# Last triangle stage: row sums on ScalarE, a given share of products for GpSimd, and a new word order

## The chip, the core and the metric

The kernel runs on one core of a Trainium2 chip. The metric is the time of one execution on the device in microseconds (us). The engines are TensorE (PE in the profile; PEld its weight loads), VectorE (DVE), ScalarE (ACT), GpSimd (POOL), and SyncE (SP), which issues most DMAs. Each works through its own instructions in program order and waits on semaphores for the others.

## The reference

Four images x of 64 x 64 x 256 go through two layers. Only the second layer's last image is touched by the change.

```python
# layer 0, per image of 4096 tokens
f, g, v = xt @ Wf + bf, xt @ Wg + bg, xt @ Wh + bh
x = x + softmax(g f^T) v @ Wo + bo
# layer 1, "triangle": 8 heads of 32, N = 64
scores = einsum('bilhd,bljhd->biljh', q, k) / sqrt(32)
att = softmax(scores, axis=2)                       # over l
out = einsum('biljh,bilhd,bljhd->bijhd', att, v1, v2)
h = layer_norm(x + out.reshape(...) @ Wo)
x = layer_norm(relu(h @ W1 + b1) @ W2 + b2 + h)
```

## The kernel before

The whole program is one list of instructions in an order written out by hand (`tc.manual_schedule()`, L1714). For each image b = 0 to 3 `layer0` (L527) makes the attention, the projections q, k, v1, v2 and the first triangle step, and then `first_layer1` (b = 0) or `next_layer1` (L1588, b = 1 to 3) makes the triangle stage. After b = 3, `Tokens.alone` (L1379) does the token work (heads, two layer norms, the two-layer perceptron) of the last image by itself; the token work of image b - 1 runs inside the triangle stage of image b.

**Steps and words.** A triangle stage has 32 steps: four pairs of heads, and eight groups of eight rows i for each. Two steps, 2i and 2i + 1, are one round of the word list. `next_layer1` goes through the list `ORDER_LAST` (for b = 3; `ORDER` for b = 1, 2) once in each of 20 periods, L1690 to L1707. A word `R14/2` is read so: letter, step of the round (1: the odd one), number, and how many periods late it is: in period p it is done for round i = p - 2. A word without a slash is for round i = p. The words, with their engine:

- `R` + step + m: product m of 8, `product` (L1067, instruction at L1078): the weights of one row and one head times v2, 128 x 2048. m of `8 - npool(step)` and above go to GpSimd (tile Rp, 2 buffers, weights from attP), the others to VectorE (tile R, 3 buffers, weights straight from att in PSUM).
- `A` + step + m: `accumulate` (L1081, L1088): TensorE sums product m over l into one of two accumulators `acc` of the step; four matmuls. It frees the R or Rp buffer.
- `T` + step + half: `take` (L1095): ScalarE copies an accumulator to SBUF; after the second one SP issues the step's eight stores.
- `S`, `W`, `V`, `t`, `c` + step: `sums` (L991: VectorE adds up the softmax rows at L1003 unless the step is in `summed`, and takes reciprocals, L1005), `weights` (L1009: ScalarE scales rows, 8 activations), `stationary` (L1051: ScalarE puts v1 into wsel; then SP loads v1 of step + 2), `turn_weights` (L1026: TensorE transposes, tile att), `copy_weights` (L1035: ScalarE copies GpSimd's part to attP).
- `K` + step: `row_sums` (L981): ScalarE makes the same row sums with 8 activations that accumulate, at L986. It is used in the first image's list, `ORDER0`, only.
- `sp`, `sf`, `e0`, `e1`, `f0`, `f1`: TensorE's scores of the next pairs (L964), and ScalarE's exponentials of them (L974); `sf` and `f` for i = 0, the others for i = 1 to 11. After that no scores are made.
- Token words of a piece q: `h0`, `h1` heads (L1196; SP then loads tiles A and yt of the next piece), `sa` statistics on VectorE (L1221), `rr` and `pp` root on ScalarE and polish on GpSimd, `fa` and `fo` affine on ScalarE (L1283), `ht` transposes on TensorE, `hT` and `hU` copies of them on ScalarE (L1311), `m0`, `m1` hidden layer on TensorE (L1339), `r0`, `r1` rectify on ScalarE (L1348), `z0`, `z1` second layer on TensorE (L1359), `so` its statistics on ScalarE (L1237, L1241), `fi` the end on GpSimd (L1373, L1374) and the output's DMA on SP.

The accumulators and the scores share two PSUM buffers (`pa`), the tiles mp, zp, hp and htp two others (`pb`). When a tile is allocated it takes the buffer that was given free first in program order, and its first writer waits for that buffer's last reader.

`npool` gives GpSimd 3 products in even and 2 in odd steps for b > 0, and goes by the string `ON_POOL` for b = 0. In the stage of b = 3 there is an exception at L1695: in the period of step 0, `A05` is left out where it stands and is done right after A04, where the list has `A04`.

```python
            if step not in self.summed:
                nc.vector.tensor_reduce(den, rows, AX.X, ALU.add)
```

Of the kernel before, what the change touches and what calls it, by code (L numbers as in the profile page):

```python
# [52 lines left out]


ORDER_LAST = """
    r0/1 A10/2 A11/2 m1/1 R14/2 R05/1 S1/1 R15/2 T10/2 sp/1 A14/2 A16/2 r1/1 e0/1 e1/1 A15/2 A05/1 T11/2 R04/1
    A04/1 z0/1 W1/1 R03/1 V1/1 fi/2 S0 z1/1 t1/1 so/1 R06/1 R00/1 c1/1 sa A03/1 R07/1 R02/1 A06/1 A02/1 A00/1
    rr/1 pp/1 W0 R01/1 A07/1 A01/1 fo/1 fa T01/1 R12/1 t0 T00/1 R17/1 h1/-1 sf/1 R13/1 h0/-1 f0/1 ht f1/1 R16/1
    hU A13/1 hT A12/1 A17/1 R11/1 c0 R10/1 m0 V0
""".split()  # L60


# [14 lines left out]


ON_POOL = "33232323332323233323232332232323"


@with_exitstack
def attention_then_triangle_kernel(
# [7 lines left out]
    NB = x.shape[0]  # L91
# [815 lines left out]
    class Layer1:  # L907
# [45 lines left out]
        def scores(self, pair, u):  # L953
            if u == 0:
                self.S[pair] = big.tile([P, N, N], F32, tag="S", name="S", bufs=2)
            qk = self.qk[pair]
            q = qk[0].rearrange("p (i l) -> p l i", l=32)
            k = qk[1].rearrange("p (l j) -> p l j", j=N)
            sp = pa("sp").rearrange("p o (l i) -> p o l i", i=N)
            for n in range(8):  # L960
                for h in range(2):
                    for lh in range(2):
                        rows = slice(64 * lh + 32 * h, 64 * lh + 32 * h + 32)
                        nc.tensor.matmul(  # L964
                            sp[ts(h, 64), lh, n, :], k[rows, u * 8 + n, :], q[rows, u * 8 + n, :],
                            start=True, stop=True,
                        )
            self.sp = (pair, u, sp)

        def take_scores(self, *halves):  # L970
            pair, u, sp = self.sp
            for lh in halves or (0, 1):
                l0 = lh * 32 + u * 8
                nc.scalar.activation(  # L974
                    self.S[pair][:, :, l0 : l0 + 8].rearrange("p i l -> p l i"), sp[:, lh],
                    AF.Copy if self.safe else AF.Exp,
                )
# [38 lines left out]
        def npool(self, step):  # L1016
            if self.b == 0:
                return int(ON_POOL[step])
            return 3 - step % 2


# [499 lines left out]
    def words_of(order):  # L1521
        for w in order:
            w, late = (w.split("/") + ["0"])[:2]
            yield w, int(late)
# [63 lines left out]
    def next_layer1(b, L, rest, ahead, F):  # L1588
        own = b == NB - 1
        t0 = NP * (b - 1)  # L1590
# [97 lines left out]
        step_word, scores, take_scores, _ = step_words(L, fetched, was_stored, spread)  # L1688
        mps[1] = {}
        for period in range(NP + 4):  # L1690
            if period == 1:
                L.owed()
            for word, late in words_of(ORDER_LAST if own else ORDER):
                i = period - late
                if own and i == 0 and word in ("A05", "A04"):  # L1695
                    for m in (4, 5) if word == "A04" else ():
                        step_word("A", 0, m)
                elif word[0] in "RATSWVtc":
                    step_word(word[0], 2 * i + int(word[1]), int(word[-1]))
                elif word in ("sp", "sf"):  # L1700
                    if (i == 0) == (word == "sf"):
                        scores(i)
                elif word in ("e0", "e1", "f0", "f1"):
                    if (i == 0) == (word[0] == "f"):
                        take_scores(i, int(word[1]))
                else:
                    of_piece(word, i)  # L1707
# [4 lines left out]
    def run(safe):  # L1712
        rest, ahead = Tokens(), Ahead()
        with tc.manual_schedule():  # L1714
            F = front0(0)
            for b in range(NB):
                L = layer0(b, F, safe, rest, ahead)
                F = Front() if b + 1 < NB else None
                if F is None:

                    rest.ios.append(L.io)
                if b == 0:
                    first_layer1(L, ahead, F)
                else:
                    next_layer1(b, L, rest, ahead, F)
                if F is not None:
                    rest.ios.append(L.io)
            rest.alone(NP * (NB - 1), NP * NB)
# [50 lines left out]
```

## Time and profile before

| what | value |
|---|---|
| median of 4 runs | 3605.39 us (3602.74 to 3607.36) |
| profiled execution, its time | 3606.98 us |
| its span, first to last instruction | 3605.1 us (1.9 us lie around it) |
| mean granted TensorE clock | 0.992 |
| busy share PE, PEld, DVE, ACT, POOL | 97%, 52%, 79%, 55%, 49% |

Busy microseconds by stage (windows of the same profile):

| stage | window, us | PE | DVE | ACT | POOL |
|---|---|---|---|---|---|
| triangle, b = 2 | 2130 to 2550 | 415.1 | 392.3 | 274.8 | 368.6 |
| attention, b = 3 | 2550 to 3000 | 442.9 | 318.1 | 209.6 | 76.9 |
| last triangle stage | 3000 to 3450 | 444.2 | 431.2 | 306.2 | 425.8 |
| of it, with scores | 3050 to 3325 | 275.0 | 266.1 | 194.1 | 264.0 |
| of it, without | 3325 to 3436 | 107.4 | 110.4 | 70.3 | 108.0 |
| tokens alone | 3450 to 3605 | 140.6 | 114.8 | 82.4 | 0 |

A busy share says how much of a window an engine was at work, not whether the others waited for it. For that one looks at the distance from one round of the word list to the next, at what each engine's idle time was ended by, and at the chain of work that ended last. The start of an instruction on one engine, set beside the end of the one it waited for on another, gives the cost of a handover.

### The profile page before, as it was taken

The page shows a single profiled execution, that of the slowest core. Times are in us where ns is not written, and L with a number is a line of the kernel's source. Part 1 is how long each engine was busy: PE and PEld are TensorE (multiplying, and loading weights), DVE is VectorE, ACT ScalarE, POOL GpSimd, SP SyncE. Part 2 cuts the span into 40 slices and gives each one's busy share as a digit, 9 for nine tenths or more (in the row PEclk, how much of TensorE's full clock was granted, in tenths as well). Part 3 has the DMA queues.
Part 4 walks back from the last instruction along what each step waited for, and adds up shares of the span by engine and source line. Part 5 has one row for each costly group of instructions (what it writes and reads, how often), then busy time and mean ns, then how long its engine had stood idle before and what let it go on. Part 6 is the DMA issues. An engine that isn't in the chain of part 4 may idle for free.

```text
span 3605.1 us, 59264 instructions
## 1 busy us (share of the span) xinstructions
PE 3509.1 (97%) x22218; PEld 1888.7 (52%) x22218; DVE 2837.1 (79%) x2620; ACT 1983.3 (55%) x4733; POOL 1755.9 (49%) x899
## 2 busy tenths in 40 slices
PE   8999999898999999999999999999999999999998
PEld 6555444444555555554555555554455555555477
DVE  4777499896555579999777749999787766999987
ACT  3444477664444366665444456666444436777655
POOL 5000099894000068889011128889511106999920
PEclk9999999999999999999999999999999999999999
DMA  9444565464222354425422264343633345341221
GB/s 171 135 134 129 131 155 144 112 148 111 68 75 69 110 133 108 109 63 107 104 91 91 76 158 103 93 100 77 126 96 103 96 110 140 92 97 46 66 69 57
DMA packets 514105, 378.60 MB, mean 105 GB/s; under 512 B 320593, under 2 KB 455505, under 8 KB 504977
## 3 DMA queue, kind: packets, MB, share of 16 engines
q1 hardware_dynamic: 464768, 347.76, 35.2%
q0 software_dynamic: 36160, 19.94, 5.4%
q10 hardware_dynamic: 12880, 7.01, 0.7%
q8 instruction: 178, 2.92, 0.3%
q14 instruction: 119, 0.97, 0.1%
HBM read 207.82 MB, written 166.72 MB: 104 GB/s over the span
## 4 chain that ended last, share of the span: by engine, by line
PE 82%; POOL 7%; DVE 5%; issue 4%; ACT 2%; DMA 1%; SPq 0%; ACTq 0%; DVEq 0%; POOLq 0%
PE o L609 24%; PE acc L1088 19%; PE proj L692 8%; PE s L582 7%; POOL Rp L1078 5%; PE mp L1339 4%; PE zp L1359 4%; PE sp L964 3%; PE v1p L724 2%; PE hp L1196 2%; PE y L661 2%; PE att L1030 1%; DVE R L1078 1%; PE vp L388 1%; PE v1p L462 1%
## 5 line engine op out<-in xcount | busy, mean ns | idle before, releaser
L1078 POOL TENSOR_TENSOR Rp<-attP,v 128x2048 f32<-128x2048 f32 x323 | 1469.1, 4580 | 407.4 <-DMA k<-k 301.5
L1078 DVE TENSOR_TENSOR R<-att,v 128x2048 f32<-128x2048 f32 x701 | 1556.1, 2279 | 67.0 <-PE acc L1088 41.1
L609 PE MATMUL o<-e,v 128*128 128x512 f32 x2048 | 1045.8, 594 | 0.0
L594 ACT ACTIVATE e<-s 128x1024 f32<-128x1024 f32 x512 | 523.0, 1023 | 529.9 <-PE s L582 446.3
L582 PE MATMUL s<-gT,fT 128*128 128x512 f32 x1024 | 788.7, 772 | 16.3 <-ACT e L594 10.9
L616 DVE TENSOR_TENSOR esum<-esum,e 128x2048 f32<-128x2048 f32 x224 | 512.4, 2287 | 305.0 <-ACT e L594 303.2
L1088 PE MATMUL acc<-R,wsel 128*32 128x512 f32 x5608 | 709.5, 602 | 19.3 <-DVE R L1078 8.4
L609 PEld LDWEIGHTS o<-e,v 128*128 128x128 f32 x2048 | 389.0, 190 | 278.1 <-issue 234.9
L1098 ACT COPY ao<-acc 128x1024 f32<-128x1024 f32 x256 | 256.7, 1011 | 259.9 <-PE acc L1088 211.9
L1088 PE MATMUL acc<-Rp,wsel 128*32 128x512 f32 x2584 | 338.0, 595 | 23.6 <-POOL Rp L1078 22.0
L1088 PEld LDWEIGHTS acc<-R,wsel 128*32 128x32 f32 x5608 | 158.2, 110 | 373.4 <-issue 276.7
L1373 POOL TENSOR_TENSOR hz<-hz,log_bc 128x512 f32<-128x512 f32 x32 | 45.7, 1427 | 599.4 <-ACT hz L1283 599.4
L582 PEld LDWEIGHTS s<-gT,fT 128*128 128x128 f32 x1024 | 195.0, 191 | 252.4 <-issue 233.6
L1013 ACT ACTIVATE es<-S,rd 128x64 f32<-128x64 f32 x1024 | 258.2, 337 | 27.2 <-DVE rd L1005 24.9
L1267 POOL TENSOR_SCALAR nt<-mv 128x2 f32<-128x2 f32 (+1 forms) x49 | 9.4, 192 | 510.4 <-DVE mv L1222 505.3
L1339 PE MATMUL mp<-hT,w 128*128 128x256 f32 x1024 | 244.8, 384 | 1.7 <-ACT hT L1311 1.7
L1359 PE MATMUL zp<-w,hid 128*128 128x256 f32 x1024 | 240.0, 385 | 2.5 <-ACT hid L1348 2.1
L1359 PEld LDWEIGHTS zp<-w,hid 128*128 128x128 f32 x1024 | 187.9, 190 | 50.1 <-issue 14.7
L1339 PEld LDWEIGHTS mp<-hT,w 128*128 128x128 f32 x1024 | 185.1, 190 | 54.8 <-ACT attP L1038 12.6
L638 DVE RECIPROCAL rec<-den 128x512 f32<-128x512 f32 x32 | 107.4, 3358 | 116.2 <-PE den L634 110.8
L1088 PEld LDWEIGHTS acc<-Rp,wsel 128*32 128x32 f32 x2584 | 79.9, 110 | 219.0 <-issue 151.0
L974 ACT ACTIVATE S<-sp 128x512 f32<-128x512 f32 x128 | 131.0, 1093 | 66.9 <-PE sp L964 66.8
(199 smaller groups left out, 3782.6 us busy)
## 6 DMA issues: line engine op xcount, KB each, us to landing
v<-v2d SPq DMA_DIRECT2D x44, 512.0 KB
v1c<-v1d SPq DMA_DIRECT2D x128, 128.0 KB
aT<-ao SPq DMA_DIRECT2D x1024, 16.0 KB
A<-aT SPq DMA_DIRECT2D x256, 64.0 KB
hz<-raw SPq DMA_DIRECT2D x32, 512.0 KB
y<-yT SPq DMA_DIRECT2D x56, 256.0 KB
q<-st SPq DMA_DIRECT2D x56, 256.0 KB
k<-st SPq DMA_DIRECT2D x52, 256.0 KB
```

Source lines behind the costliest of these rows:

```text
L582: nc.tensor.matmul(s_ps[r // 2][:, r % 2, :], fT[tt][:, ts(r * 4 + n, P)], gT[qb // 4][:, ts(qb % 4, QB)], start=True, stop=not safe,)
L594: nc.scalar.activation(e[g][:, 2 * j : 2 * j + 2, :], s_ps[j], AF.Exp)
L609: nc.tensor.matmul(o_ps[qb], F.v[tt][:, r * 4 + n, :], es[:, r, :], start=(k == 0 and r == 0), stop=(k == 7 and r == 3),)
L616: nc.vector.tensor_tensor(esum[qb], esum[qb], es, ALU.add)
L692: nc.tensor.matmul(ps, w[:, cc, rows], y(qb, cc), start=(cc == 0), stop=(cc == 1))
L974: nc.scalar.activation(self.S[pair][:, :, l0 : l0 + 8].rearrange("p i l -> p l i"), sp[:, lh], AF.Copy if self.safe else AF.Exp,)
L1013: nc.scalar.mul(e[:, i, :], rows[:, i, :], rec[:, i : i + 1])
L1078: eng.tensor_tensor(R, src.unsqueeze(1).to_broadcast([P, D, N]), v2[h], ALU.mult)
L1088: nc.tensor.matmul(acc[32 * c : 32 * c + 32, n % 2, :], w[:, n, c, 16 * h : 16 * h + 32], R[:, ts(c, 8), :].rearrange("p d j -> p (d j)"), ...
L1098: nc.scalar.copy(self.ao[step][:, ts(np, 2)].rearrange("p k d j -> p k (d j)"), self.acc[step][np])
L1339: nc.tensor.matmul(self.mp[:, fc % 2, :], w1_sb[:, cc, ts(fc, P)], self.hT[tt][:, cc, :], start=(cc == 0), stop=(cc == 1),)
L1359: nc.tensor.matmul(zp[:, n, :], self.hid[tt][:, fc, ts(n, P)], w2_sb[:, fc, :], start=(fc == 0), stop=(fc == 3 and tt not in self.hT2),)
```

## The change

Three things change, all in the stage of b = 3. The list `ORDER_LAST` is a new one; it has the words K0 and K1, so that steps 1 to 31 get their row sums from ScalarE (step 0 is done in `layer0`, as before); the heads h0 and h1 are no longer made one period early. `npool` goes by a new string, 79 products in all instead of 80. The exception for `A05` and `A04` is gone. The number of all other instructions stays.

```diff
 ORDER_LAST = """
-    r0/1 A10/2 A11/2 m1/1 R14/2 R05/1 S1/1 R15/2 T10/2 sp/1 A14/2 A16/2 r1/1 e0/1 e1/1 A15/2 A05/1 T11/2 R04/1
-    A04/1 z0/1 W1/1 R03/1 V1/1 fi/2 S0 z1/1 t1/1 so/1 R06/1 R00/1 c1/1 sa A03/1 R07/1 R02/1 A06/1 A02/1 A00/1
-    rr/1 pp/1 W0 R01/1 A07/1 A01/1 fo/1 fa T01/1 R12/1 t0 T00/1 R17/1 h1/-1 sf/1 R13/1 h0/-1 f0/1 ht f1/1 R16/1
-    hU A13/1 hT A12/1 A17/1 R11/1 c0 R10/1 m0 V0
+    R14/2 A12/2 A17/2 c0/1 hU/1 R16/2 R05/1 K0 m0/1 m1/1 A11/2 A16/2 S1/1 R04/1 A14/2 R15/2 S0 V0/1 r0/1 R01/1
+    T10/2 A05/1 A04/1 W1/1 A15/2 K1 r1/1 R07/1 h0 R02/1 h1 T11/2 z1/1 V1/1 z0/1 W0 R00/1 R06/1 t1/1 fi/2 so/1
+    A02/1 A01/1 A07/1 A06/1 A00/1 sa c1/1 rr/1 R03/1 pp/1 T01/1 A03/1 sf/1 T00/1 sp fa R10/1 R13/1 t0 f1/1 f0/1
+    e1 ht e0 hT A10/1 R12/1 A13/1 R17/1 R11/1 fo/1
 """.split()
...
 ON_POOL = "33232323332323233323232332232323"
+ON_POOL_LAST = "32323322332323232323213232332322"
...
         def npool(self, step):
             if self.b == 0:
                 return int(ON_POOL[step])
+            if self.b == NB - 1:
+                return int(ON_POOL_LAST[step])
             return 3 - step % 2
...
             for word, late in words_of(ORDER_LAST if own else ORDER):
                 i = period - late
-                if own and i == 0 and word in ("A05", "A04"):
-                    for m in (4, 5) if word == "A04" else ():
-                        step_word("A", 0, m)
-                elif word[0] in "RATSWVtc":
+                if word[0] in "RATKSWVtc":
                     step_word(word[0], 2 * i + int(word[1]), int(word[-1]))
```

## The prediction

> **What bounds the kernel now.** First the table of stages (columns: window, its length, then busy microseconds of PE, PEld, DVE, ACT, POOL, clock, DMA share, GB/s). Only the last triangle stage, about 3000 to 3450 us, is touched; one row from its middle and one from its end:
>
> ```profile
> 3225.00:3250.00 25.00, 25.00 (x240) 13.23 (x232) 24.10 (x19) 18.53 (x51) 23.86 (x14) 1.00 0.59 135
> ...
> 3375.00:3400.00 25.00, 24.12 (x176) 11.31 (x177) 24.93 (x16) 17.24 (x52) 24.35 (x14) 1.00 0.33 82
> ```
>
> TensorE has no gap in the middle; at the end VectorE and GpSimd have none. Next the chain that ended last (start, duration, what), to see how long one period of the word list is and who sets it:
>
> ```profile
> 3050.57 0.86 PE hp L1196 x4
> ...
> 3078.33 0.86 PE hp L1196 x4
> ...
> 3353.65 6.80 POOL Rp L1078 x2
> ...
> 3380.84 6.80 POOL Rp L1078 x2
> ```
>
> The period is 27.76 while scores (`sp`) are made, all on PE; without scores it is 27.19, on POOL, though PE's work is 1.91 less (25.85). So in the middle relief of VectorE buys nothing; an order that is cheaper for PE does.
>
> Then the timelines of PE, DVE and ACT, for the handovers:
>
> ```profile
> 3155.67 1.07 PE L1088 MATMUL acc<-R,wsel 128*32 128x512 f32 x8
> 3156.55 1.04 PE L1088 MATMUL acc<-Rp,wsel 128*32 128x512 f32 x8
> ...
> 3159.99 1.04 PE L1088 MATMUL acc<-R,wsel 128*32 128x512 f32 x8
> 3160.96 0.66 PE L1030 MATMUL att<-ident,es 128*128 128x128 f32 x4
> ```
>
> ```profile
> 3156.80 13.28 DVE L1078 TENSOR_TENSOR R<-att,v 128x2048 f32<-128x2048 f32 x6 [0.35 <-PE acc L1088]
> ...
> 3327.78 8.88 DVE L1078 TENSOR_TENSOR R<-att,v 128x2048 f32<-128x2048 f32 x4
> ...
> 3348.10 15.45 DVE L1078 TENSOR_TENSOR R<-att,v 128x2048 f32<-128x2048 f32 x7
> ```
>
> ```profile
> 564.22 0.26 ACT L986 ACTIVATE S<-S 128x64 f32<-128x64 f32 x1
> 564.37 0.20 ACT L986 ACTIVATION_READ_ACCUMULATOR S<-S 128x1 f32 x1
> 564.46 0.25 ACT L986 ACTIVATE S<-S 128x64 f32<-128x64 f32 x1
> ```
>
> An accumulation costs PE 0.86 from start to start, 0.97 before another kind. A03's matmuls end at 3156.55; R01, which needs its buffer, starts 0.25 later. Four products take VectorE 8.88, seven 15.45 (2.21 each). A product that is done is used 0.03 later (R02: 3348.10 + 2.29 = 3350.39, A02 at 3350.42). A row sum on ScalarE takes 0.24, accumulator read included: 1.92 a step.
>
> **Row sums.** 31 reductions leave VectorE (0.71 to the next start; step 0's stays): 1.42 a period; a period without waits goes from 27.1 to 11 x 2.21 + 1.16 (bn_stats) + 0.24 (reciprocals) = 25.7. ScalarE gains 3.84 a period: 70.6% of 27.76, or 19.6, becomes 23.4. Queued behind the K words are r0, T10, W1 and r1; I walk them below.
>
> **GpSimd's share.** 79 products instead of 80, five in every period but one, which has four. Its loop stays 5 x 4.55 + 2.60 (finish) + 1.85 (polish) = 27.2.
>
> **PE's new order.** A12 A17 m0 m1 A11 A16 A14 A05 A04 A15 h0 h1 z1 z0 t1 A02 A01 A07 A06 A00 A03 sp t0 ht A10 A13, then A12 again. The accumulations stand in three runs instead of four (0.11 less) and m0, m1 stand together: sixteen of their matmuls in the last stage take 3.46 (3466.92 to 3470.38), so an m costs 1.73 and 1.92 only before another kind (0.19 less); the z pair comes after transposes, 1.95 each as the second is now (3153.19 to 3155.14), 0.10 less in all. Sum: runs 3.55 + 5.29 + 5.29, m 3.65, h 2.16, z 3.90, sp 1.91, t and ht 1.52 = 27.3 with scores, 25.4 without.
>
> A rule speaks on PE's share. The Trainium skill, "Perfetto Trace Analysis", Identifying the Most-Contended Engine, says that matmul busy time is no measure of the distance to the limit and that weight-load busy time is better; in the first row above that is 13.23 of 25, which would leave PE about half free. The trace sides with it in part only: the 0.11 and 0.19 show that "100%" can shrink, but the starts lie end to end. By the rule alone PE would drop out of the sum and GpSimd's 27.2 would be the period.
>
> **The new tightest loop.** VectorE's products run R14, R05 or R15 with R04, R01, R02, R00, bn_stats, R03, R10, R13, R12, R11. With three R buffers, R03 in the built program waits for A02's last matmul. From A02's end: 0.25, R03 R10 R13 R12 8.88, 0.03, so A12 can start at 9.16. PE's own way there (A01 A07 A06 A00 A03 sp t0 ht A10 A13) is 9.0 with scores, 7.1 without. From A12's start to the next A02's end: 0.86 + 0.97 + 3.65 + 5.29 + 2.16 + 3.90 + 0.53 + 0.86 = 18.2. The loop is 27.4, **with or without scores**. bn_stats is not in it: h1 is done 5 us before A02's end.
>
> Walked through it, counting from A02's end: ScalarE ends fa at 6.4 (ht can then start at 6.6; with scores it comes at 6.8), fo at 10.3 (m0 at 11.0), T10 at 16.7 (A05 at 17.2), r1 at 21.3 (z1 at 22.0), W0 at 25.1 (t0 a period on at 33.7). GpSimd polishes at 1.4 to 3.3, R17 to 7.8 (A17 at 10.0), R16 to 12.4 (A16 at 15.5), R05 or R15 to 16.9 (A05 17.2, A15 18.9), and ends finish 1.1 into the next period: 0.2 spare. In periods with R15 on GpSimd, R04 waits for A11 and is ready as A04 wants it (18.1): nothing spare. SP's queue keeps all its issues, 14.5 of 27.4 (two stores of about 5.2, tiles A and yt 2.5, others 1.4); the output leaves at about 1.5 and lands by 5, hU needs its buffer at 10.4; A and yt have 25 us to land.
>
> **Start.** Step 1's sum waits for ScalarE: K1 begins where W1 now does (3005.26), ends 3007.2, and R04, queued behind that reciprocal, starts 4.4 later than now. PE does A05 first (GpSimd's product, ready 3007.67), A04 at 3009.7, then z1, z0, t1, which cover the delay of W1; K0, K1 and W0 lie under them. A02 of pair 0 ends at 3016.1 instead of 3015.8: +0.3. To A02 of pair 1: 27.3 + 1.9 (two scores) + 0.3 (R03) = 29.5, now 31.4: -1.9. If the z words did not cover, the bound is the whole 4.4 later start; the other bound is 0.
>
> **Periods.** Ten with scores: 10 x (27.4 - 27.76) = -3.6. Four without: 4 x 27.4 = 109.6 against 107.6 now (3324.0 to 3431.6): +2.0. VectorE's relief is eaten by the wait for A02.
>
> **End.** Now 17.4 from the last A02 (3432.5) to the heads of the next stage (3449.91). New: 9.16 + 0.86 + 0.97 + 3.65 + 3.55 + 1.73, the last for piece 17's heads, which are no longer made early: 19.9: +2.5. Their statistics then follow at once, so the next stage's first hidden matmul waits about 0.6 longer.
>
> Sum: 0.3 - 1.9 - 3.6 + 2.0 + 2.5 + 0.6 = -0.1. The profiled execution (3606.98 with span 3605.1) would become 3606.9; on the median of the runs, 3605.39, I forecast **3605.3**. About 0.2%, 7.2 us, is what a measurement of this kernel can tell from no change.
>
> **Rivals.** *Slower: VectorE's loop is longer than I have it.* R03's buffer comes one accumulation later (A01), or handovers add as much: for it, VectorE idles about 1.7 before R03 in every period and two loops have nothing spare; against it, the wait in the built program. It costs 0.86 x 14 = 12: **3617**. It decides from 0.5 a period (7.2 / 14). GpSimd gets there too if a product takes 0.15 more than 4.55 (27.95). Chance 0.20.
> *Faster: PE's work alone sets the pace.* Then 10 x (27.3 - 27.76) - (107.6 - 4 x 25.4) = -4.6 - 6.0, end 0 instead of +2.5: sum -11.6: **3594**. For it, VectorE has 1.4 less; against it, three buffers. Chance 0.12.
> *The change does not do what it says*: the dispatch list now has K, and 31 reductions are gone from the built program; were they still there, each period would be 1.4 fuller on VectorE, inside its idle time: about 3605. Chance below 0.02, counted with the forecast.
>
> Forecast case 0.68. Unknown terms: loop 14 x 0.15, start 1.5, end 1.5, so about 3 either way alone; to leave out no more than 2 in 10 the range goes part of the way to both rivals: **3598 to 3614**. Faster by over 0.2% 0.12, within 0.68, slower 0.20.
>
> **What would show it.** Heads to heads 27.4 in both halves of the stage; VectorE waiting about 1.7 for PE before R03 every period; PE waiting about 2 at A12 once the scores are gone; reductions 97 to 66, 248 more row-sum activations on ScalarE, GpSimd products 323 to 322; the next stage starting within 3 us of 3450. Periods above 27.9, or a wait of PE at A04, A05, z1 or ht, would make me wrong on the slow side; periods near 25.4 without scores on the fast side.

## The result, and the profile after

| | before | after |
|---|---|---|
| median, us | 3605.81 (60 runs, 3602.74 to 3608.25) | 3610.05 (40 runs, 3606.27 to 3613.36) |
| ratio | | 1.0012, 95% interval 1.0007 to 1.0016 |
| profiled execution: time, span | 3606.98, 3605.1 | 3612.13, 3610.3 |

The time is inside the range on record and within 0.2%. But the change is slower by more than the interval of its ratio, and I had forecast no change (a sum of -0.1). So the sum is wrong by about 4 us in the medians and by 5.3 in the two profiles, and the question is which terms were wrong.

The change did what it says: VectorE's reductions went from 97 to 66, ScalarE's row-sum activations from 248 to 496, GpSimd's products from 323 to 322, and the next stage starts at 3452.7.

Now the two windows that were shown of before. Columns: window, length, busy time of PE, PEld, DVE, ACT, POOL, clock, DMA share, GB/s:

```profile
3225.00:3250.00 25.00, 25.00 (x242) 12.60 (x240) 22.94 (x16) 20.45 (x68) 23.95 (x14) 1.00 0.63 134
3375.00:3400.00 25.00, 23.38 (x177) 10.90 (x176) 22.99 (x17) 18.77 (x77) 24.01 (x15) 1.00 0.42 110
```

VectorE is relieved as intended (24.10 to 22.94, and 24.93 to 22.99) and ScalarE has the work. TensorE still has no gap in the middle, and at the end now no engine is full: a sign that a chain over several engines sets the pace there. Its length is read from the heads (PE's timeline of after, first instruction of each pair):

```profile
3231.39 1.13 PE L1199 MATMUL hp<-wo,A 128*128 128x256 f32 x4
...
3259.00 1.13 PE L1199 MATMUL hp<-wo,A 128*128 128x256 f32 x4
...
3286.61 1.13 PE L1199 MATMUL hp<-wo,A 128*128 128x256 f32 x4
...
3315.61 1.13 PE L1199 MATMUL hp<-wo,A 128*128 128x256 f32 x4
...
3343.17 1.13 PE L1199 MATMUL hp<-wo,A 128*128 128x256 f32 x4
```

The period is 27.61 or 27.56 in both halves (before: 27.76 with scores, on average 26.9 without), and one period is 29.00. Which of the two it is follows the string of GpSimd's share: 27.61 where GpSimd has R15, so that VectorE makes R05 ahead of R04, and 27.56 where GpSimd has R05. PE's and VectorE's timelines show A02, and behind it the predicted wait before R03, in brackets behind the instruction:

```profile
3155.26 1.92 PE L1091 MATMUL acc<-R,wsel 128*32 128x512 f32 x16
```

```profile
3156.39 15.48 DVE L1081 TENSOR_TENSOR R<-att,v 128x2048 f32<-128x2048 f32 x7 [1.92 <-PE acc L1091]
```

A02 (the first eight of the sixteen) starts at 3155.26 and ends 0.88 later; R03 follows after 0.25. So the loop that I named exists. Without scores one sign came out otherwise than I had written: TensorE's wait stands at ht, for ScalarE's h, and not at A12 (PE's timeline):

```profile
3357.28 0.66 PE L1309 MATMUL htp<-ident,h 128*128 128x128 f32 x4 [1.47 <-ACT h L1286]
...
3359.94 1.06 PE L1091 MATMUL acc<-R,wsel 128*32 128x512 f32 x8 [0.15 <-DVE R L1081]
```

A12 still starts 9.19 after A02's end (I had 9.16), so behind the wait for h only 0.15 is left of the wait for VectorE: two chains end there almost together.

Set side by side from A02 to A02 and on to the next stage's first hidden matmul, in the two profiles:

| term | predicted | profiled |
|---|---|---|
| start, to A02 of pair 0 (3014.97, now 3015.61) | +0.3 | +0.6 |
| pair 0 to pair 1 (31.39, now 29.31) | -1.9 | -2.1 |
| ten periods with scores (277.6, now 277.4) | -3.6 | -0.2 |
| four without (107.6, now 109.9) | +2.0 | +2.3 |
| last A02 to the next stage's first hidden matmul (25.25, now 29.51) | +3.1 | +4.3 |
| from there to the end of the span (148.2, now 148.6) | 0 | +0.4 |
| sum | -0.1 | +5.2 (rounded terms give 5.3) |

Two terms failed: the ten periods with scores (3.4 off), one of which is the period of 29.00, and the end (1.2 off). The rest is within 0.4.

In the period of 29.00 TensorE waits for VectorE and GpSimd stands idle (timelines of PE, VectorE and GpSimd):

```profile
3312.57 1.04 PE L1091 MATMUL acc<-R,wsel 128*32 128x512 f32 x8
3314.62 1.06 PE L1091 MATMUL acc<-R,wsel 128*32 128x512 f32 x8 [1.00 <-DVE R L1081]
```

```profile
3310.07 4.49 DVE L1081 TENSOR_TENSOR R<-att,v 128x2048 f32<-128x2048 f32 x2
```

```profile
3304.68 13.64 POOL L1081 TENSOR_TENSOR Rp<-attP,v 128x2048 f32<-128x2048 f32 x3 [3.08 <-ACT attP L1041]
```

The list has A05, A04, A15 and then the heads. A04 (3312.57) waits for nothing; the accumulation with the wait of 1.00, the last ahead of the heads at 3315.61, is A15. It waits for R15, which VectorE makes there behind R16 and R04 and ends at 3314.56.

At the end, the clock (windows, columns as above; then PE's timeline):

```profile
3437.00:3441.00 4.00, 1.94 (x20) 0.71 (x16) 4.00 (x3) 2.62 (x5) 4.00 (x2) 1.00 0.27 86
3441.00:3444.50 3.50, 3.50 (x21) 0.80 (x17) 3.50 (x3) 2.15 (x5) 3.50 (x1) 0.51 0.11 23
3444.50:3448.00 3.50, 3.50 (x24) 2.38 (x17) 3.50 (x2) 0.50 (x2) 3.42 (x3) 1.00 0.02 5
```

```profile
3273.92 2.91 PE L1091 MATMUL acc<-R,wsel 128*32 128x512 f32 x24
...
3439.62 0.66 PE L1309 MATMUL htp<-ident,h 128*128 128x128 f32 x4 [2.06 <-ACT h L1286]
3440.20 4.48 PE L1091 MATMUL acc<-R,wsel 128*32 128x512 f32 x24
```

TensorE waits 2.06 for ScalarE's h, and shortly after it works at half the clock (0.50 for 3.41 us; the window of 3.50 has 0.51 on average). Three accumulations (x24) take 4.48; in a period they take 2.91 (the first line). A busy PE (3.50 of 3.50) hides this: only the clock column tells it.

### The profile page after: what moved, and what is told of

It is laid out like the page before. It is cut to its first block, busy times and chain, and to the rows that moved or that the text cites. A ratio compares the mean times of both kernels' runs of the same rounds, so it can differ in the third digit from the quotient of the medians.

```text
span 3610.3 us, 59790 instructions
## 1 busy us (share of the span) xinstructions
PE 3505.1 (97%) x22218; PEld 1888.7 (52%) x22218; DVE 2819.0 (78%) x2590; ACT 2038.1 (56%) x5229; POOL 1749.5 (48%) x898
```

## The experiments

Each kernel was timed beside the kernel before; its ratio is to that. Earlier stages differ by up to 4 us between profiles of the same code (the stage's first heads come at 3000.8 to 3004.8), so I also give "rest": from those heads to the end of the span in the profile. "Period" is the distance between rounds with scores and without, the one long period (below) left out; "27.6" stands for 27.56 and 27.61, by GpSimd's share as above. "Fall" says whether the clock fell to 0.50 around the end of the stage.

| kernel | median, us | ratio (95%) | rest, us | period | fall |
|---|---|---|---|---|---|
| before | 3605.81 | | 601.1 | 27.76, 26.9 | no |
| after | 3610.05 | 1.0012 (1.0007 to 1.0016) | 606.3 | 27.6, 27.6 | yes |
| a06_first | 3622.82 | 1.0052 (1.0038 to 1.0066) | 618.3 | 28.42 and 28.46, the same | no |
| swap | 3608.12 | 1.0008 (0.9999 to 1.0017) | 602.8 | 27.43 and 27.48, 27.2 to 27.5 | no |
| a02_early | 3621.77 | 1.0043 (1.0029 to 1.0057) | 616.6 | 28.0 and 28.8, the same | yes |
| a02_before_t1 | 3611.41 | 1.0017 (1.0008 to 1.0026) | 606.2 | 27.76, 27.5 to 27.6 | no |
| sums_on_dve | 3615.71 | 1.0030 (1.0018 to 1.0043) | 609.7 | 27.56 and 28.20, the same | no |
| sums_only | 3626.74 | 1.0062 (1.0048 to 1.0076) | 623.2 | 29.4, 27.5 | no |
| sums_only_2 | 3610.50 | 1.0015 (1.0006 to 1.0024) | 604.7 | 27.76, 26.9 | no |
| npool_old | 3606.19 | 1.0004 (0.9995 to 1.0013) | 603.6 | 27.56, 27.56 | yes |
| pool21 | 3608.27 | 1.0008 (0.9999 to 1.0017) | 603.2 | 27.6, 27.6 | no |
| early_heads | 3607.18 | 1.0006 (0.9997 to 1.0015) | 602.4 | 27.6, 27.6 | no |
| warm | 3608.21 | 1.0012 (1.0003 to 1.0021) | 604.8 | 27.6, 27.6 | no |
| step1_dve | 3608.44 | 1.0009 (1.0000 to 1.0018) | 603.4 | 27.6, 27.6 | no |
| best2 | 3604.34 | 0.9998 (0.9989 to 1.0007) | 600.3 | 27.43 and 27.48, 27.2 to 27.5 | no |
| best3 | 3603.63 | 0.9997 (0.9988 to 1.0006) | 598.6 | 27.48, 27.48 | no |

The kernel before's own median lay between 3604.86 and 3605.77 from one session to the next, so medians of different kernels can be set side by side to about 1 us. The intervals of swap, a02_before_t1, npool_old, pool21, early_heads, warm and step1_dve overlap that of the changed kernel. For these the distances in the profiles carry the argument, and a median can only agree.

### Is the loop from A02 the pace? a06_first and swap

```diff
-    A02/1 A01/1 A07/1 A06/1 A00/1 ...
+    A06/1 A02/1 A01/1 A07/1 A00/1 ...
```

> The changed kernel with A06 done ahead of A02 instead of behind A07; TensorE's work is the same, A02 starts one accumulation (0.86) later. Theory (the two loops from A02): every period grows by 0.86 with and without scores, to 28.5, and the end by 0.86: 14 x 0.86 + 0.9 = 13 slower, 3623. Rival 1 (TensorE's own work or GpSimd's 27.2 sets the pace): 27.6 as it is, 3610. Rival 2 (only the loop of the periods without scores binds): 4 x 0.86 + 0.9 = 4.3 slower, 3614.3.

The heads of a06_first (PE's timeline), one pair with scores and one without:

```profile
3237.05 1.13 PE L1199 MATMUL hp<-wo,A 128*128 128x256 f32 x4
...
3265.51 1.13 PE L1199 MATMUL hp<-wo,A 128*128 128x256 f32 x4
...
3380.67 1.13 PE L1199 MATMUL hp<-wo,A 128*128 128x256 f32 x4
...
3409.13 1.13 PE L1199 MATMUL hp<-wo,A 128*128 128x256 f32 x4
```

28.46 in both halves for 27.61, and 28.42 for 27.56: the 0.86, to 0.01, for an order in which TensorE does the same work. So the loop had no slack to take it up. The rest grew by 12.0 (without a fall, which the changed kernel's profile has), the median by 12.8. Both rivals fall. This is the clearest run of all: delaying one instruction of a suspected loop by a known amount and seeing each period grow by that amount.

```diff
-    R14/2 A12/2 A17/2 c0/1 ...
+    R14/2 A17/2 A12/2 c0/1 ...
-    ... A05/1 A04/1 W1/1 A15/2 K1 ...
+    ... A05/1 A15/2 A04/1 W1/1 K1 ...
```

> The changed kernel with two pairs of words exchanged: A17 ahead of A12 and A15 ahead of A04; the same work, each of the two accumulations that wait for VectorE comes 0.86 later. Theory (the loops A02 - R03 R10 R13 R12 - A12 and A02 - R03 ... R04 - A04 hold 27.62, with TensorE's own work of 27.5 and the chain A03 - T00 - fa - ht just below): with scores 27.5, without about 27.25 (the ht chain and GpSimd's 27.2), the end 0.3 shorter: 2 to 3.5 less than the changed kernel, 3606.5 to 3608. Rival 1 (TensorE's own work is 27.6 already): only the four periods without scores gain, 1.5. Rival 2 (GpSimd's products R17 and R15 come too late for their earlier places): 27.8 or more, 3612.

In the other direction it worked too: 27.43 (heads of swap, PE's timeline), the rest 3.5 less, of which 1.4 is the fall that its profile does not have.

```profile
3230.22 1.13 PE L1199 MATMUL hp<-wo,A 128*128 128x256 f32 x4
...
3257.65 1.13 PE L1199 MATMUL hp<-wo,A 128*128 128x256 f32 x4
```

So TensorE's own work is at most 27.43 (I had 27.3), and the loop held the period 0.1 to 0.2 above it.

### A shorter loop by an earlier A02: two misses

```diff
-    ... z1/1 V1/1 z0/1 W0 R00/1 R06/1 t1/1 fi/2 so/1 A02/1 A01/1 A07/1 ...
+    ... z1/1 V1/1 A02/1 A01/1 z0/1 W0 R00/1 R06/1 t1/1 fi/2 so/1 A07/1 ...
```

> The changed kernel with A02 and A01 done between z1 and z0, 2.5 us earlier in TensorE's order; nothing else moves. Theory (VectorE's loop from A02 over R03 R10 R13 R12 to A12 holds the period at 27.6): VectorE's wait of 1.9 before R03 shrinks below 0.5; periods with scores stay near TensorE's own 27.5 to 27.6 (one more change between kinds of matmul), periods without scores fall from 27.58 to GpSimd's 27.2 (4 x 0.4 = 1.5), the end gets 1.9 shorter: 3 to 4 us less than the changed kernel, about 3606.5. Rival (GpSimd or TensorE's own work already holds 27.6): no period changes by more than 0.1 and the time stays within 1 us of 3610.0.

It got 12 slower than the changed kernel. VectorE's timeline says why:

```profile
3158.45 2.26 DVE L1081 TENSOR_TENSOR R<-att,v 128x2048 f32<-128x2048 f32 x1
3163.03 13.28 DVE L1081 TENSOR_TENSOR R<-att,v 128x2048 f32<-128x2048 f32 x6 [2.32 <-ACT attP L1041]
```

R03 is early now, but R10 behind it waits 2.32 for c1, which on ScalarE stands behind `so`, which waits for z0, which I had pushed back. The wait was removed in one place and came back in another; "nothing else moves" in my expectation was wrong.

```diff
-    ... t1/1 fi/2 so/1 A02/1 A01/1 A07/1 ...
+    ... fi/2 so/1 A02/1 A01/1 t1/1 A07/1 ...
```

> The changed kernel with t1 done after A02 and A01 instead of ahead of them; A02 is 0.53 earlier and no word of another engine moves. Theory (two loops through VectorE's buffers, A02 - R03 R10 R13 R12 - A12 and A02 - R03 ... R04 - A04, both 27.62, hold the period): both get 0.53 shorter; with scores TensorE's own work of 27.5 to 27.6 remains, without scores GpSimd's 27.2 (4 x 0.4 = 1.6 less), the end 0.5 less: 1 to 2.5 less than the changed kernel, 3607.5 to 3609. Rival (loops do not bind): within 0.5 of 3610.0, periods without scores still 27.5 or more.

No gain. With scores the period is 27.76 and, the long period aside, TensorE waits for nothing: transposes in the middle of the accumulations cost it two changes of kind. Without scores, ht, which hangs on A03, T00 and fa, moved back as far as A02 moved forward. The chain over ht and TensorE's own work lie within 0.3 of the loop, so shortening one thing alone gains little.

### Row sums: sums_on_dve, sums_only, sums_only_2, step1_dve

sums_on_dve drops the words K0 and K1 from the new list.

> The changed kernel without the words K0 and K1: the 31 row sums are VectorE's reductions again, the order of all else and GpSimd's share are the new ones. Theory (the relief of VectorE went into its wait for A02): the reductions' 1.42 a period fill the wait of 1.9 before R03, the period stays at 27.6, the stage start is up to 0.6 earlier; 3608.5 to 3611. Rival 1 (VectorE's fill sets the period, so the row sums on ScalarE are worth 1.42 a period): 14 x 1.42 = 20 us slower, 3630. Rival 2 (the K words delay ScalarE's copies and rectifications): 0.2 a period faster, 3606 to 3607.

Neither the theory nor rival 1 had it. PE's and VectorE's timelines:

```profile
3175.41 1.07 PE L1091 MATMUL acc<-R,wsel 128*32 128x512 f32 x8 [0.43 <-DVE R L1081]
```

```profile
3172.29 0.68 DVE L1004 TENSOR_REDUCE dens<-S 128x8 f32<-128x512 f32 x1
3173.00 0.20 DVE L1006 RECIPROCAL rd<-dens 128x8 f32<-128x8 f32 x1
3173.12 2.24 DVE L1081 TENSOR_TENSOR R<-att,v 128x2048 f32<-128x2048 f32 x1
```

One of the two reductions stands between R05 and R04, in the second loop (A02, R03 ... R04, A04), which has no slack: R04 ends at 3175.36 and A04 starts at 3175.41. That one reduction costs 0.6 a period (28.20 for 27.61), the other disappears in the wait before R03. This holds in the nine periods of fourteen in which GpSimd has R15 and VectorE makes R05 ahead of R04. In those in which GpSimd has R05 the period is 27.56 with the reductions as without them. So 0.6 of VectorE's 1.42 is needed in nine periods, and nothing of it in the others: it is the new share that makes the row sums worth something. With the old share, which leaves R05 to GpSimd in every round, they should buy nothing in the periods; no run shows that.

sums_only and sums_only_2 go the other way: the kernel before, with K words alone.

```diff
-    ... V1/1 fi/2 S0 z1/1 t1/1 so/1 R06/1 R00/1 c1/1 ... m0 V0
+    ... V1/1 K0 fi/2 z1/1 t1/1 so/1 R06/1 R00/1 S0 c1/1 ... m0 V0 K1
```

> The kernel before with nothing but K words added (K0 and S0 placed where ScalarE and VectorE idle, K1 ahead of r0): row sums on ScalarE in the old order, GpSimd's 80 products as before. Theory (in the old order TensorE holds 27.76 with scores and GpSimd 27.2 without, so VectorE's 1.42 a period buys nothing): within 1.5 us of the kernel before, 3604.3 to 3606.5. Rival 1 (VectorE held the periods without scores): 4 x 0.7 to 4 x 1.4 less, 3600 to 3603. Rival 2 (K words in ScalarE's queue delay r0 or so by 0.3 or more a period): 3609 or more.

This one measures a bad place, not the row sums: VectorE's reciprocal waits for K0 in every period.

```profile
3193.01 0.20 DVE L1005 RECIPROCAL rd<-dens 128x8 f32<-128x8 f32 x1 [3.12 <-ACT S L986]
```

With K0 right behind e1 instead, and S0 where it was:

```diff
-    ... e0/1 e1/1 A15/2 ... m0 V0
+    ... e0/1 e1/1 K0 A15/2 ... m0 V0 K1
```

> The kernel before with nothing but K words added, at other places than in sums_only: K0 right behind e1, K1 ahead of r0; S0 stays where it is. Theory (in the old order TensorE holds 27.76 with scores and GpSimd 27.2 without; the 20 us of sums_only were the wait of VectorE's reciprocal for K0, 3.1 a period): within 1.5 us of the kernel before, 3604 to 3607. Rival 1 (VectorE's fill held part of it): 3600 to 3603. Rival 2 (3.84 us more on ScalarE cannot be placed in the old order without a wait of TensorE or VectorE): 3610 or more.

By its time rival 2 would be right, but its periods are those of the kernel before, with scores (27.76) and without (25.85, 26.88, 27.22, 26.80 from A03 to A03; before 25.85, 26.84, 27.19, 26.81). Of the 3.6 in the rest 3.4 is lost ahead of pair 1, where ScalarE makes 16 sums before W1 (PE's timeline, then the windows):

```profile
3008.40 1.28 PE L1088 MATMUL acc<-R,wsel 128*32 128x512 f32 x8 [3.78 <-ACT es L1013]
```

```profile
3009.00:3013.00 4.00, 4.00 (x20) 1.72 (x10) 4.00 (x4) 1.25 (x6) 2.82 (x2) 0.57 0.98 229
```

Here too the clock fell after the wait. So the row sums alone buy nothing in the old order's periods, as predicted.

step1_dve is the changed kernel with K left out for step 1 alone.

> The changed kernel with one of the 31 row sums, that of step 1, made by VectorE again. Theory (at the stage's start R04 stands behind a reciprocal that waits for ScalarE's sums of step 1, until 3007.3; VectorE is idle there): R04 starts with the stage's first products, A04 does not wait, z1 comes up to 1.5 earlier; 0.5 to 1.5 less than the changed kernel, 3608.5 to 3609.5. Rival (what follows waits for VectorE's next products anyway): 3610.

The first z1 comes 1.5 earlier (5.49 instead of 7.03 after the heads); 0.6 of that is lost again before the z1 of pair 1 (29.98 instead of 29.42). The median, 1.6 lower, agrees.

### GpSimd's share: npool_old and pool21

npool_old puts `3 - step % 2` back.

> The changed kernel with GpSimd's old share, three products in even and two in odd steps (80 in all); K words and order are the new ones. Theory (GpSimd has 0.2 to 0.3 to spare in each period of five products, and the share of single steps moves no bound): within 1.5 of the changed kernel, 3608.5 to 3611.5, periods 27.6. Rival (the step-by-step share is what lets the new order run, R15 or R05 comes too late without it): 0.3 or more in each second period, 3612.5 or more.

Its median is 3.9 lower (by the ratios 2.9), and its rest 2.7, though both profiles have the fall; the theory missed that. Its periods are 27.56 throughout, with no 29.00. In the string of the changed kernel, step 21 has a 1, so that period leaves VectorE twelve products. pool21 alters that figure alone:

```diff
-ON_POOL_LAST = "32323322332323232323213232332322"
+ON_POOL_LAST = "32323322332323232323223232332322"
```

> The changed kernel with one figure of GpSimd's string altered: step 21 gets 2 products instead of 1 (80 in all). Theory (in the changed kernel one period of 29.0 among those of 27.6 is the one in which step 21 leaves a twelfth product to VectorE; A04 waits 1.0 for R04 while GpSimd idles 3.1): that period falls to 27.6, and the time by 1.4, to 3608 to 3609. Rival 1 (the period is long because the scores end there): it stays at 29.0, 3610. Rival 2 (all of the 3.9 that the old share gained came from this one figure): 3606 to 3607.

```profile
3284.11 1.13 PE L1199 MATMUL hp<-wo,A 128*128 128x256 f32 x4
...
3311.67 1.13 PE L1199 MATMUL hp<-wo,A 128*128 128x256 f32 x4
```

The period (heads of pool21, PE's timeline) is 27.56 instead of 29.00, and the median 1.8 lower (by the ratios 1.4): the single figure is the cause. My expectation named the wrong accumulation, though: it is A15 that waits for R15, as the lines of the result show, and not A04 for R04. swap agrees, since with A15 one accumulation earlier its long period is 29.72, or 2.3 above its others instead of 1.4. In the profiles the other figures of the string add 0.05 in each of the nine periods that have R15 on GpSimd (27.61 against 27.56), 0.4 in all. The further gain of npool_old's median over pool21's (2.1, by the ratios 1.4) is larger than that, its interval overlaps pool21's, and I leave it open.

### The end: early_heads and warm

```diff
...
+                elif own and word == "ht" and period == n0 - 2:
+                    of_piece("h0", n0 - 1)
+                    of_piece("h1", n0 - 1)
+                    of_piece(word, i)
```

(The heads of piece 17 take a buffer of `pc`, and are not done again in the last period.)

> The changed kernel with the heads of piece 17 alone (two words, once) moved from the last period to just ahead of ht in the last period but one, where TensorE waits 2.06 us for ScalarE; their tile comes from the PSUM buffers of att. Theory (end: heads no longer made early cost their 1.73, and the wait of 2.06 let the granted clock fall to 0.50 for 3.4 us, which cost 1.4): 1.7 less from the heads, 1.4 less where the clock had fallen, statistics earlier: 2 to 3.5 us less than the changed kernel, 3606.5 to 3608, and a clock of 1.00 throughout the window from 3430 to 3460. Rival (the end is VectorE's products and what follows them, the heads lie beside): within 0.7 of 3610.0.

The heads now fill the wait (PE's timeline):

```profile
3432.76 1.90 PE L1091 MATMUL acc<-R,wsel 128*32 128x512 f32 x16
3434.59 2.00 PE L1200 MATMUL hp<-wo,A 128*128 128x256 f32 x8
3436.72 0.66 PE L1310 MATMUL htp<-ident,h 128*128 128x128 f32 x4
```

The clock stayed at 1.00, the rest is 3.9 shorter and the median 2.9 lower. To part the two causes, warm fills the same wait with idle work:

```diff
...
+                    fill = pc("fill")
+                    for k in range(16):
+                        nc.tensor.transpose(fill[:, ts(k % 4, P)], ident, ident)
...
```

> The changed kernel with 16 transposes of a constant into a PSUM tile that nobody reads, once, just ahead of ht in the last period but one, where TensorE waits 2.06 us for ScalarE; work is added and nothing else changes. Theory (that wait let the granted clock fall to 0.50 for 3.4 us and A12 and its neighbours ran at half pace): the clock stays at 1.00 from 3430 to 3460, the next stage's first hidden matmul comes 1.4 us earlier; in time 0.5 to 1.5 us less than the changed kernel, 3608.5 to 3609.5, since not every run need have had the fall. Rival (the fall is not due to that wait, or lies beside the path): clock as it was, or no earlier start; 3610.

```profile
3434.30:3438.30 4.00, 3.84 (x36) 2.44 (x32) 4.00 (x3) 2.65 (x5) 4.00 (x2) 1.00 0.28 85
3438.30:3441.80 3.50, 3.35 (x30) 0.92 (x23) 3.50 (x3) 2.13 (x5) 3.50 (x1) 1.00 0.13 28
```

No fall, and the next stage's first hidden matmul comes 456.2 after the first heads instead of 457.7. That is the cost of a fall, 1.4; early_heads has 454.2, so the earlier heads gain another 2.0. But warm does not show that the filler kept the clock up. Nine kernels have this wait of 2.05 or 2.06 without a filler, and only three of them (the changed kernel, npool_old, a02_early) show the fall. In time warm and the changed kernel can't be told apart (1.0012 each, intervals 0.0018 and 0.0009 wide).

The traces show what parts the three from the six. In each of the 16 profiles all clock changes of the execution (14 to 20) lie on a grid with a step of 3.413 us, and the grid lies differently in each execution. In the grid step that is emptiest around the wait, TensorE is busy for 1.41 of 3.41 us in the changed kernel (window 3437.62 to 3441.03) and for 1.36 in npool_old and a02_early, and the clock falls for just the next step. In the other six it is busy for 1.45 (swap), 1.60 (sums_on_dve), 1.78 (pool21, a02_before_t1), 1.95 (a06_first) and 2.36 (step1_dve): more of the step is busy, or the wait straddles two steps. In warm's own grid the step would have 1.60 without the filler, and in early_heads the wait would straddle two steps, so neither was due to fall. The fall thus belongs to the single execution; if the grid lies anywhere alike, the wait falls into one step in about (3.41 - 2.06) / 3.41 = 0.4 of them, an estimate. The border between 1.41 and 1.45 is seen at this place only: with other work, at about 640 us, steps with up to 2.4 us busy are followed by a fall as well.

The Trainium skill, "TensorE: Matmul & The Clock Gate", Part 1: The HAM clock gate, says that the clock is halved after an idle window of about 3.4 us, and that the windows run freely, not from the kernel's start. The grid, its step and its lying differently in each execution agree with that. The idle window does not quite: the step ahead of the fall was not idle, TensorE was busy for 1.41 of 3.41.

### Putting it together: best2 and best3

best2 has swap, early_heads and step1_dve; best3 has GpSimd's old share as well.

> The changed kernel with swap, early_heads and step1_dve together. Theory: their gains add up, 2.5 + 3 + 1 = 6.5 less than the changed kernel, 3603.5, which is 1 to 3 less than the kernel before. Rival (they draw on the same slack): 3605 to 3607, no faster than the kernel before.

> The changed kernel with GpSimd's old share, the two exchanges of swap, early_heads and step1_dve together. Theory: best2 without its one period of 29.7 (27.4 instead) is 2.3 less than best2, 3601.5 to 3602.5, faster than the kernel before by 0.1%. Rival (without the string's other figures R15 or R05 on GpSimd come too late for the exchanged order): 3604 or more.

best2 has a period of 29.72, best3 none over 27.48 behind the first. best3's rest is 2.5 shorter than that of the kernel before and 7.7 shorter than that of the changed one, its median 1.4 below before of the same session (0.9988 to 1.0006). Against the changed kernel best3's gain is clear. That it beats the kernel before is seen in the profile only; the times can't tell.

## Why the prediction was wrong

- **"What bounds the kernel now", "Start", pair 0 to 1: right.** Each of these terms came out within 0.4, the loop is the one named, and it runs with or without scores. a06_first shows that it is the pace, sums_only_2 that the row sums alone buy nothing in the middle.
- **"Periods. Ten with scores": the failed step.** I priced all ten alike at 27.4 and had -3.6; the profile has -0.2. One of the ten (1.4) was priced wrongly, and all of them (2.0) were a little too short; the next two points have them.
- **"GpSimd's share": the wait that was not priced.** I counted "five in every period but one, which has four" and priced GpSimd's loop alone. A product that GpSimd does not do is done by VectorE: in that period VectorE makes R16 as well as R15, and R15 comes late for A15. My walk through the period has A15 at 18.9 with R15 as GpSimd's product, and never the period with twelve products of VectorE. That period is 29.0, 1.4 too long (pool21).
- **"The new tightest loop", 27.4: right mechanism, wrong size.** It is 27.6. From A12's start to A02's end I had 18.2, and it is 18.4: 0.11 more for the heads, which now follow accumulations instead of transposes (2.27, not 2.16), and where VectorE makes R05 0.05 more for the run of six (5.34, not 5.29). A sum of transitions borrowed from another order was short by 0.2, and ten periods make 2.0 of it. The rival "VectorE's loop is longer" was this, at a quarter of its price; I had put its point of decision at 0.5 a period.
- **"Four without", +2.0, measured +2.3: right in part by luck.** Three of the four have the same 0.2 too much (27.56, 27.56, 27.61). The last is 27.16, since its heads take 1.83 instead of 2.27, which I had not counted. The wait of about 2 that I expected at A12 stands at ht (1.47), one of the places that I had named as signs of being wrong. It cost little, as the walk had ht's start right (6.6, measured 6.5 after A02's end).
- **"VectorE's relief is eaten by the wait for A02": partly wrong.** In nine of the periods 0.6 of the 1.42 is what lets A04 keep its place (sums_on_dve), and 0.8 is eaten; where GpSimd has R05 all of it is.
- **"End", +2.5 +0.6: right apart from the clock.** 3.1 predicted, 4.3 in the profile, 2.7 to 3.0 where the clock held (27.99 to 28.20 in pool21, warm and step1_dve, less 25.25). I had no term for the clock.
- **The faster rival** (TensorE's own work alone, 3594) fell: a06_first shows the wait for VectorE's buffer at work, though no run gave VectorE a fourth one. Even swap, which relaxes the loops, reaches 27.43 only. The rule of the Trainium skill that I weighed ("Perfetto Trace Analysis", Identifying the Most-Contended Engine: go by the weight loads, by which TensorE is half free) would have made GpSimd's 27.2 the period; no run with scores came below 27.43.

The sizes add up: 2.0 (loop) + 1.4 (twelfth product) + 1.4 (clock) + 0.4 (behind the last stage) = 5.2 of the 5.3 by which the sum missed. In the medians, where the fall does not come in each run, the miss is 4.3. What made the 0.4 behind the last stage is open.

## What to carry to other kernels

When a share of work is shifted between two engines step by step, price each period for both engines: the one that gets a unit more can be the one on the loop. To test a suspected loop, delay one instruction of it by a known time and look whether every period grows by just that; taking a wait away, as a02_early did, mixes in whatever else moves. And a tuned order has several chains within a few tenths of a microsecond of each other, so that one edit gains little, and the gain comes from relaxing them together.

## What the runs showed of the hardware that I had not expected

- A wait of 2.06 of TensorE was followed by 3.4 us at half clock in three of nine profiles, 1.4 us on the path where it came. They are the three in which one step of a grid of 3.413 us, which lies differently in each execution, has TensorE busy for 1.41 us or less; with 1.45 (swap) the clock held. A longer wait at the stage's start (3.78, sums_only_2) was followed by a fall too.
- The order of the kinds of matmul has a price of its own: with t1 in the middle of the accumulations TensorE took 27.76 without a wait, and with t1 ahead of them (swap) 27.43.
- The same code reached the last stage up to 4 us apart in different profiles, so single spans of this kernel cannot be compared to better than that; distances inside one stage agree to 0.05.
